# A perceiver layer on one core: another order for the first loads, the first layer norm and queries, and the combining of the weights

## The chip, the core and the metric

The kernel runs on one core of a Trainium2 chip. TensorE (PE) does the matmuls, VectorE (DVE), ScalarE (ACT) and GpSimd (POOL) the elementwise work, and SyncE (SP) issues nearly all loads. Each engine takes its instructions in the order in which the program lists them, and waits at an instruction until the semaphores that it names have been raised. The metric is the device time of one execution in microseconds (us). Before the change it is 3820.44 us (median of three runs, 3818.95 to 3823.2).

## What is computed

Sixteen sequences of 128 rows with 512 channels pass through cross attention over a context of 2048 rows each, a state space block with an MLP, and a small gated feed-forward. The change touches the first of the three:

```python
x = x + _L0_xattn_ref(_layernorm(x, axis=-1), ctx_1024, ...)
...
q = queries @ wq.T + bq
k = context @ wk.T + bk
v = context @ wv.T + bv
...
attn = jnp.einsum('bhnd,bhsd->bhns', q, k) * scale
attn = jax.nn.softmax(attn, axis=-1)
out = jnp.einsum('bhns,bhsd->bhnd', attn, v)
...
return out @ wo.T + bo
```

All values are float32.

## The kernel before, in words

**Blocks and units.** The context of each sequence is cut into four blocks of 512 rows. A block `g` yields keys (`kts`) and values (`vts`), and four units `u`, one for each group of four heads, work on it: scores (L299), maxima (L307), exponentials (L317), transposes (L330), weighted values (L343). The main loop runs over the units, and what belongs to the next block, the state space block and the MLP is put between them by tables written out by hand.

**Products.** Keys and values of a block are 512x512x512 products, made by a scheme with seven half-size products in place of eight. Weights and context are held as quarters of 2x256 columns. Four differences of context quarters, `t1` to `t4`, are formed on GpSimd (`ctx_sums`, L229), and four combinations of weight quarters, `s1` to `s4`, on VectorE (`weight_sums`, L213 to L216), the latter once for keys (`ks`) and once for values (`vs`). `product` (L237) makes one of the seven as eight passes of TensorE. They come in two phases, each in two steps: `x_products` and `y_products`. Phase 0 has products 1 and 2 in the first step, which take loaded quarters alone (`a11` with `c00`, `a12` with `c10`), and product 6 in the second; phase 1 has 7 and 5, then 3 and 4. Between them ScalarE copies a result out of PSUM (`hold`), and VectorE adds it to another (`k_sum` L257, `v_sum` L267).

**The beginning.** For block 0 there is no loop to hide in: loads, sums and products are listed one after another behind the tables (from L1128 on). SyncE's queue holds x of sequence 0 (L174), then keys' four weight quarters (L203), four context quarters (L154), values' four weight quarters, the four rows of the output projection `wo` (L169), the four columns of the query weights `wq` (L167), and the context of block 1. `wo` and `wq` share a ring of six buffers, so the last two of `wq` wait until TensorE has read two of `wo`. GpSimd issues ten small loads at the same time. All SyncE transfers of this stage are 256 KB.

The first loads are followed by the two phases of products for keys and values, with values in banks 0 and 1 of PSUM and keys in `pa` and `pc`. Then a projection of values' bias by `wo` (L464, called with `bvx`) goes to bank 2, and VectorE adds it to `bo` (L1154). Then come layer norm of sequence 0 (`moments_of`, `root_of`, `normal`: L66 to L91, L83 and L84 on ScalarE, L373), in which GpSimd adds `bo` to x (L376), the transposes of the normed rows (L385) with their copy to `xnT` (L387), and the queries (L395) with their copies to `qT` (L404). The first scores need `qT` and `kts`.

Of the kernel before, what the change touches and what calls it, by code (L numbers as in the profile page):

```python
# [10 lines left out]
ALU = mybir.AluOpType  # L11
# [23 lines left out]
def perceiver_layer(ctx: ExitStack, tc: tile.TileContext, a: dict, out: bass.AP):  # L35
    nc = tc.nc
# [72 lines left out]
    with ExitStack() as es:  # L109
# [15 lines left out]
        banks = [psum.tile([P, 512], FP, tag=f"s{j}", name=f"bank{j}") for j in range(4)]  # L125
        avp = psum.tile([P, 4, P], FP, tag="av", name="avp")
        hst = psum.tile([P, NH // 2, GT], FP, tag="h0", name="hst")
        pa = psum.tile([P, 2, 256], FP, tag="pa", name="pa")
        pc = psum.tile([P, 2, 256], FP, tag="pc", name="pc")
# [4 lines left out]
        bo = row_in(acon, "bo")  # L134
# [3 lines left out]
        ctx_t, kts, vts, qts, prs, pts, avs, stats, xts = ({} for _ in range(9))  # L138
# [5 lines left out]
        def halves(ps):  # L144
            return ps.rearrange("p (k q) -> p k q", q=256)

        def load_ctx(g, names=("c00", "c10", "c11", "c01")):

            for n in names:
                j, c = int(n[1]), int(n[2])  # L150
                t = pool.tile(
                    [P, 2, 256], FP, tag=n, name=f"{n}_{g}", bufs=1 if n == "c01" else 2
                )
                nc.sync.dma_start(  # L154
                    t,
                    a["ctxT"][g // SB, g % SB][
                        :, 2 * j : 2 * j + 2, c * 256 : (c + 1) * 256
                    ],
                )
                ctx_t[g, j, c] = t  # L160

        def load_w(i, b):

            for c in range(KC):
                t = ssm.tile([P, KC, P], FP, tag="ws", name=f"wqo{i}_{b}_{c}", bufs=WS)
                if i == 0:
                    nc.sync.dma_start(t, a["wqkvo"][i][:, :, c * P : (c + 1) * P])  # L167
                else:
                    nc.sync.dma_start(t.rearrange("p a b -> p (a b)"), a["wqkvo"][i][:, c, :])  # L169
                wts_in[i, b, c] = t  # L170

        def load_x(b):
            t = keep.tile([P, D], FP, tag="x", name=f"x{b}", bufs=4)
            nc.sync.dma_start(t, a["x"][b])  # L174
            xts[b] = t
# [20 lines left out]
            7: ("s3", "t3"),  # L196
        }

        def load_factors(of, i):

            for o, j, name in ((0, 0, "a11"), (0, 1, "a12"), (1, 1, "a22"), (1, 0, "s3")):
                t = pool.tile([P, 2, 256], FP, tag=of + name, name=of + name, bufs=1)
                nc.sync.dma_start(  # L203
                    t, a["wqkvo"][i][:, 2 * j : 2 * j + 2, o * 256 : (o + 1) * 256]
                )
                wfac[of, name] = t

        def weight_sums(of):
            a11, a12, a22, s3 = (wfac[of, n] for n in ("a11", "a12", "a22", "s3"))
            for n in ("s1", "s2", "s4"):  # L210
                wfac[of, n] = pool.tile([P, 2, 256], FP, tag=of + n, name=of + n, bufs=1)
            s1, s2, s4 = (wfac[of, n] for n in ("s1", "s2", "s4"))
            nc.vector.tensor_tensor(s1, s3, a22, ALU.add)  # L213
            nc.vector.tensor_tensor(s2, s1, a11, ALU.subtract)
            nc.vector.tensor_tensor(s3, a11, s3, ALU.subtract)
            nc.vector.tensor_tensor(s4, a12, s2, ALU.subtract)  # L216

        def ctx_sums(g, names):
            b11, b12, b21, b22 = (ctx_t[g, j, c] for j in range(2) for c in range(2))
            for n in names:  # L220
                t = pool.tile([P, 2, 256], FP, tag=n, name=f"{n}_{g}", bufs=1)
                cfac[g, n] = t
                x, y = {
                    "t1": lambda: (b12, b11),
                    "t2": lambda: (b22, cfac[g, "t1"]),
                    "t3": lambda: (b22, b12),
                    "t4": lambda: (b21, cfac[g, "t2"]),
                }[n]()
                nc.gpsimd.tensor_tensor(t, x, y, ALU.subtract)  # L229
# [41 lines left out]
        def x_products(of, g, ph, pa, pc):  # L271
            for i, ps in (((1, pa), (2, pc)), ((7, pa), (5, pc)))[ph]:
                product(of, g, i, ps)

        def hold(key, g, pa, tag):
            t = pool.tile([P, 2, 256], FP, tag=tag, name=f"{tag}{key}{g}", bufs=1)
            nc.scalar.copy(t, pa)
            held[key] = t

        def x_sums(of, g, ph, pa, pc):  # L280
            sums[of](g, ph, ph, pc, held[of])

        def y_products(of, g, ph, pa, pc):
            for i, ps in (((6, pa),), ((3, pc), (4, pa)))[ph]:
                product(of, g, i, ps)

        def y_sums(of, g, ph, pa, pc, tag="u2"):
            if ph == 0:
                hold(of + "u2", g, pa, tag)
            else:  # L290
                sums[of](g, 0, 1, pc, held[of + "u2"])
                sums[of](g, 1, 0, None, pa)
# [68 lines left out]
        def moments_of(b):  # L361
            moments(keep, mv[:, b, :], xts[b])
            xts[b, "r"] = root_first(keep, mv[:, b, 1:2], 1e-5)

        def root_of(b):
            root_second(*xts[b, "r"])

        def normal(b):

            x = xts[b]  # L370
            root_third(rstd[:, b : b + 1], *xts.pop((b, "r")))
            xn = keep.tile([P, D], FP, tag="aT", name="xn", bufs=1)
            nc.vector.tensor_scalar(  # L373
                xn, x, mv[:, b, 0:1], rstd[:, b : b + 1], ALU.subtract, ALU.mult
            )
            nc.gpsimd.tensor_tensor(x, x, bo, ALU.add)  # L376
            xts[b, "n"] = xn
            nm = [keep.tile([P, SB, 4], FP, tag=f"nm{j}", name=f"nm{b}_{j}") for j in range(4)]
            sm = keep.tile([P, SB, H], FP, tag="sm", name=f"sm{b}")
            stats[b] = nm, sm  # L380

        def turned(b, ps):
            xn = xts.pop((b, "n"))
            for kc in range(KC):
                nc.tensor.transpose(heads(ps)[:, kc, :], xn[:, kc * P : (kc + 1) * P], ident)  # L385
            xnT = keep.tile([P, KC, P], FP, tag="fx", name="xnT")
            nc.vector.tensor_copy(xnT, heads(ps))  # L387
            xts[b, "t"] = xnT

        def queries(b, ps):  # L390
            xnT = xts.pop((b, "t"))
            for oc in range(KC):
                wq = wts_in.pop((0, b, oc))
                for kc in range(KC):
                    nc.tensor.matmul(  # L395
                        heads(ps)[:, oc, :],
                        wq[:, kc, :],
                        xnT[:, kc, :],
                        start=(kc == 0),
                        stop=(kc == KC - 1),  # L400
                    )
            qT = pool.tile([P, KC, P], FP, tag="qT", name=f"qT{b}")
            for oc in range(KC):
                nc.scalar.activation(  # L404
                    qT[:, oc, :],
                    heads(ps)[:, oc, :],
                    AF.Identity,
                    bias=bq[:, oc : oc + 1],
                    scale=scale,
                )  # L410
            qts[b] = qT
# [714 lines left out]
            put(late, NU - 1, lambda ps, b=b: turned_in(xrs[b], b, "mT", ps))  # L1126


        load_x(0)
        load_factors("k", 1)  # L1130
        load_ctx(0)
        load_factors("v", 2)
        load_w(3, -1)
        nc.scalar.preload_act_table_set("natural_log_exp_and_others")
        nc.scalar.activation(aneg, aneg, AF.Exp)
        nc.vector.tensor_scalar_mul(aneg, aneg, -1.0)

        bvx = keep.tile([P, KC, P], FP, tag="fx", name="bvx")
        nc.vector.tensor_copy(bvx, bv.unsqueeze(2).to_broadcast([P, KC, P]))
        ctx_sums(0, ("t1", "t2", "t3", "t4"))  # L1140
        weight_sums("k")
        weight_sums("v")
        ways = (("k", pa, pc, "u2"), ("v", halves(banks[0]), halves(banks[1]), "u2v"))
        for ph in range(2):
            for of, sa, sc, tag in ways:
                x_products(of, 0, ph, sa, sc)
                hold(of, 0, sa, "u1")
                x_sums(of, 0, ph, sa, sc)
            for of, sa, sc, tag in ways:
                y_products(of, 0, ph, sa, sc)  # L1150
                y_sums(of, 0, ph, sa, sc, tag)
        ps = banks[2]
        out_proj(bvx, -1, ps)
        nc.vector.tensor_tensor(bo, bo, ps, ALU.add)  # L1154
        load_w(0, 0)
        load_ctx(1)
        moments_of(0)
        root_of(0)
        normal(0)
        turned(0, banks[3])  # L1160
        queries(0, banks[2])
        anew(hst)

        last = 32 * NG + LAG + 32 + 4
# [164 lines left out]
```

## Time and profile before

| | |
|---|---|
| median of three runs | 3820.44 us |
| the profiled execution's own time | 3821.1 us |
| its span | 3819.3 us |
| mean granted TensorE clock | 0.993 |
| TensorE busy from 0 to 57.60 us, before the first scores | 39.10 us |
| VectorE, ScalarE, GpSimd busy in that stretch | 18.50, 7.25, 18.84 us |
| mean rate of loads in that stretch | 142 GB/s |

The span is the time on the device from the first to the last instruction that the profiler recorded; the execution's own time holds what lies around it as well. In the timeline a row names the start in us, the length in us, the engine, the line, the operation and the tiles (written, then read), and in brackets how long the engine had been idle and what ended that. Rows of one group are merged ("x8" are eight passes), and matmuls are pipelined, so neighbouring rows overlap. A row of a window of time gives, in this order, its length, the busy time (with the number of instructions) of PE, PE's weight loads, DVE, ACT and POOL, then the granted TensorE clock, the share of DMA engines that were busy, and GB/s.

### The profile page before, as it was taken

To read this page: it belongs to the slowest core of one execution; us is meant where nothing else is said; L and a number is where in the kernel's file an instruction comes from. 1 tells how busy PE (TensorE), PEld (TensorE's weight loads), DVE (VectorE), ACT (ScalarE), POOL (GpSimd) and SP (SyncE) were. 2 spreads that over 40 slices of the span, in tenths; PEclk is the share of its full clock that TensorE was granted. 3 is DMA by queue.
4 is the path that set the end of the run, shared out by engine and by line. 5 is a ranking of instruction groups with operands and counts; after the bars stand their busy time and mean duration, and the time that the engine had idled before them with its cause. 6 is when DMAs were issued, how large, how long until landed. Compare 5 with 4: busy or idle time off the path is not lost.

```text
span 3819.3 us, 70341 instructions
## 1 busy us (share of the span) xinstructions
PE 3747.7 (98%) x26120; PEld 2856.3 (75%) x26120; DVE 2711.8 (71%) x4852; ACT 2445.3 (64%) x5847; POOL 2104.1 (55%) x1968
## 2 busy tenths in 40 slices
PE   7999999999999999999999999999999989999999
PEld 6878787778777877788778877787878766656555
DVE  3444444887878787878788778877887777677843
ACT  3555556777767776777677767776777665545421
POOL 1111113676657666765666666666675667567730
PEclk9999999999999999999999999999999999999999
DMA  3111122444353435343534453445444447577752
GB/s 92 39 38 42 45 75 65 145 141 155 121 172 133 158 119 182 130 155 115 188 125 147 129 191 123 145 131 179 135 157 131 158 169 272 193 263 257 264 191 72
DMA packets 341223, 548.40 MB, mean 144 GB/s; under 512 B 24432, under 2 KB 225408, under 8 KB 340624
## 3 DMA queue, kind: packets, MB, share of 16 engines
q1 hardware_dynamic: 340464, 543.28, 42.9%
q8 instruction: 206, 3.38, 0.3%
q14 instruction: 137, 1.12, 0.1%
q0 software_dynamic: 416, 0.63, 0.1%
HBM read 527.29 MB, written 16.52 MB: 142 GB/s over the span
## 4 chain that ended last, share of the span: by engine, by line
PE 84%; DVE 9%; ACT 3%; issue 2%; DMA 1%; POOL 1%; SPq 0%; DVEq 0%; ACTq 0%; POOLq 0%
PE pa L237 21%; PE pc L237 15%; PE bank L330 10%; PE bank L299 7%; PE avp L343 6%; PE bank L518 5%; PE bank L865 3%; PE bank L699 3%; DVE hst L670 2%; PE bank L834 2%; PE bank L960 2%; DVE nm L307 2%; PE bank L395 2%; DVE w L673 2%; PE bank L464 1%
## 5 line engine op out<-in xcount | busy, mean ns | idle before, releaser
L307 DVE TENSOR_REDUCE nm<-bank 128x1 f32<-128x512 f32 x1024 | 634.6, 681 | 251.1 <-PE bank L299 250.2
L686 POOL TENSOR_TENSOR ysum<-ysum,w 128x512 f32<-128x512 f32 x384 | 500.5, 1303 | 483.4 <-DVE hst L649 303.0
L317 ACT ACTIVATE pr<-bank,nm 128x512 f32<-128x512 f32 x1024 | 689.7, 687 | 94.6 <-DVE nm L307 89.1
L635 POOL TENSOR_TENSOR w<-dx,bc 128x512 f32<-128x512 f32 x512 | 649.7, 1290 | 3.8
L335 ACT COPY pT<-bank 128x512 f32<-128x512 f32 x816 | 437.8, 585 | 222.3 <-PE bank L330 218.1
L670 DVE TENSOR_TENSOR_SCAN hst<-hst,w 128x512 f32<-128x512 f32 x456 | 556.9, 1221 | 12.3 <-ACT hst L656 8.5
L330 PE MATMUL bank<-ident,pr 128*128 128x128 f32 x4096 | 525.8, 275 | 16.4 <-ACT pr L317 14.5
L656 ACT ACTIVATE hst<-dt,alog 128x254 f32<-128x254 f32 x912 | 436.5, 479 | 147.3 <-DVE hst L649 128.7
L330 PEld LDWEIGHTS bank<-ident,pr 128*128 128x128 f32 x4096 | 472.7, 142 | 74.7 <-ACT pr L317 22.3
L343 PEld LDWEIGHTS avp<-pT,v 128*32 128x32 f32 x8192 | 208.0, 109 | 193.7 <-issue 193.7
L673 DVE TENSOR_TENSOR w<-hst,bc 128x512 f32<-128x512 f32 x456 | 315.1, 691 | 23.7 <-DMA bc<-bcd 8.3
L299 PE MATMUL bank<-kt,qT 32*128 32x512 f32 x2048 | 297.2, 640 | 6.1 <-DVE avs L458 5.6
L229 POOL TENSOR_TENSOR t<-c,c 128x512 f32<-128x512 f32 x128 | 164.4, 1284 | 251.6 <-PE pc L237 244.4
L343 PE MATMUL avp<-pT,v 128*32 128x128 f32 x8192 | 276.7, 276 | 0.0
L237 PE MATMUL pa<-t,ks 128*128 128x256 f32 x1024 | 248.7, 386 | 0.0
L237 PE MATMUL pa<-vs,t 128*128 128x256 f32 x1008 | 244.7, 386 | 0.0
L518 PE MATMUL bank<-zT,win 128*128 128x256 f32 x968 | 222.0, 383 | 4.6 <-ACT hs L848 4.6
L237 PEld LDWEIGHTS pa<-vs,t 128*128 128x128 f32 x1008 | 185.4, 190 | 34.7 <-issue 10.1
L317 ACT ACTIVATION_READ_ACCUMULATOR pr<-bank,nm 128x1 f32 x1024 | 209.5, 205 | 0.0
L237 PEld LDWEIGHTS pa<-t,ks 128*128 128x128 f32 x1024 | 184.7, 190 | 32.6 <-issue 10.5
L333 DVE COPY pT<-bank 128x512 f32<-128x512 f32 x208 | 143.8, 691 | 89.3 <-PE bank L330 87.8
L518 PEld LDWEIGHTS bank<-zT,win 128*128 128x128 f32 x968 | 181.5, 192 | 28.7 <-ACT hs L848 5.0
(301 smaller groups left out, 6849.8 us busy)
## 6 DMA issues: line engine op xcount, KB each, us to landing
bc<-bcd SPq DMA_DIRECT2D x512, 512.0 KB, 4.3
c<-in_ctxT_dram SPq DMA_DIRECT2D x256, 256.0 KB, 4.2
wf<-in_w_dram SPq DMA_DIRECT2D x128, 512.0 KB, 7.1
wqo<-in_wqkvo_dram SPq DMA_DIRECT2D x128, 256.0 KB, 4.8
win<-in_win_dram SPq DMA_DIRECT2D x128, 256.0 KB, 4.5
wout<-in_wout_dram SPq DMA_DIRECT2D x128, 256.0 KB, 4.0
x<-in_x_dram SPq DMA_DIRECT2D x16, 256.0 KB, 3.7
x1d<-x SPq DMA_DIRECT2D x16, 256.0 KB, 2.2
```

The lines of the kernel that those rows point to most:

```text
L237: nc.tensor.matmul(ps[:, r, :], l[:, kc, r * P : (r + 1) * P], m[:, kc, :], start=(i in (1, 2, 5) and r == 0 and kc == 0), stop=(r == 1 an ...
L299: nc.tensor.matmul(banks[j], qts[b][rows, hg, :], kts[u // 4, hg][rows, :], start=True, stop=True)
L307: nc.vector.tensor_reduce(stats[b][0][j][:, sb, hg : hg + 1], banks[j], AX.X, ALU.max, negate=True)
L317: nc.scalar.activation(pr[:, j, :], banks[j], AF.Exp, bias=nm[j][:, sb, hg : hg + 1], accum_out=sm[:, sb, h : h + 1],)
L330: nc.tensor.transpose(ps[:, j, :], prs[u][:, j, i * P : (i + 1) * P], ident)
L335: nc.scalar.copy(pT, ps)
L343: nc.tensor.matmul(avp[j * HD : (j + 1) * HD, hg, :], vts[u // 4, hg // 2, i // 2][:, i % 2, hg % 2 * P + j * HD : hg % 2 * P + (j + 1) * HD],
L518: nc.tensor.matmul(ps, w[:, kc, :], zTs[g][:, kc, :], start=(kc == 0), stop=(kc == KC - 1))
L635: nc.gpsimd.tensor_tensor(w, dx.unsqueeze(1).to_broadcast([P, NH // 2, GT]), bcs[g * 32 + r, 0][:, i * NH // 2 : (i + 1) * NH // 2, :], AL ...
L656: nc.scalar.activation(bt(h[:, k, :])[:, :, 1:], bt(dt)[:, :, 1:], AF.Exp, scale=aneg[:, ec, n : n + 1],)
L670: nc.vector.tensor_tensor_scan(flat, flat, w.rearrange("p n t -> p (n t)"), 0.0, ALU.mult, ALU.add)
L686: nc.gpsimd.tensor_tensor(s, s, w, ALU.add)
```

## The change

The beginning for block 0 is listed in another order; no instruction is added or taken away.

- SyncE's queue: keys' `a11`, context `c00`, keys' `a12`, context `c10`, x, values' `a11` and `a12`, context `c11` and `c01`, keys' `s3` and `a22`, values' `s3` and `a22`, the four of `wq`, then the four of `wo`. `load_factors` takes the names of the quarters to load. Now the last two of `wo` wait for buffers of `wq`.
- Layer norm of sequence 0 stands behind the first step of keys' products, ahead of their sums.
- The first step of values' products stands ahead of the context differences and of all weight combinations. Keys' weights are combined first, then come values' first sums, and then values' weights are combined.
- Transposes and queries stand behind values' weights, ahead of the second step of phase 0. In VectorE's order the copy to `xnT` follows values' combinations; in TensorE's order the queries follow the transposes and precede product 6.
- The exponential of `alog`, its sign and `bvx` follow the queries.
- The load of `wo` follows the second step of phase 0. The projection of values' bias stays behind phase 1.
- For sequence 0 GpSimd's addition of `bo` to x leaves `normal` and follows VectorE's sum for `bo`.

From the first scores on, each engine has the same instructions in the same order as before.

```diff
-        def load_factors(of, i):
-
-            for o, j, name in ((0, 0, "a11"), (0, 1, "a12"), (1, 1, "a22"), (1, 0, "s3")):
+        QUARTERS = {"a11": (0, 0), "a12": (0, 1), "s3": (1, 0), "a22": (1, 1)}
+
+        def load_factors(of, i, names):
+
+            for name in names:
+                o, j = QUARTERS[name]
...
-            nc.gpsimd.tensor_tensor(x, x, bo, ALU.add)
+            if b:
+                nc.gpsimd.tensor_tensor(x, x, bo, ALU.add)
...
+        ways = (("k", pa, pc, "u2"), ("v", halves(banks[0]), halves(banks[1]), "u2v"))
+
+        def first_products(of, ph):
+            x_products(of, 0, ph, *dict((w[0], w[1:3]) for w in ways)[of])
+
+        def first_sums(of, ph):
+            sa, sc = dict((w[0], w[1:3]) for w in ways)[of]
+            hold(of, 0, sa, "u1")
+            x_sums(of, 0, ph, sa, sc)
+
+        load_factors("k", 1, ("a11",))
+        load_ctx(0, ("c00",))
+        load_factors("k", 1, ("a12",))
+        load_ctx(0, ("c10",))
         load_x(0)
-        load_factors("k", 1)
-        load_ctx(0)
-        load_factors("v", 2)
-        load_w(3, -1)
+        load_factors("v", 2, ("a11", "a12"))
+        load_ctx(0, ("c11", "c01"))
+        load_factors("k", 1, ("s3", "a22"))
+        load_factors("v", 2, ("s3", "a22"))
+        load_w(0, 0)
         nc.scalar.preload_act_table_set("natural_log_exp_and_others")
+        first_products("k", 0)
+        moments_of(0)
+        root_of(0)
+        normal(0)
+        first_sums("k", 0)
+        first_products("v", 0)
+        ctx_sums(0, ("t1", "t2", "t3", "t4"))
+        weight_sums("k")
+        first_sums("v", 0)
+        weight_sums("v")
+        turned(0, banks[3])
+        queries(0, banks[2])
         nc.scalar.activation(aneg, aneg, AF.Exp)
         nc.vector.tensor_scalar_mul(aneg, aneg, -1.0)
+        for of, sa, sc, tag in ways:
+            y_products(of, 0, 0, sa, sc)
+            y_sums(of, 0, 0, sa, sc, tag)
+        load_w(3, -1)
 
         bvx = keep.tile([P, KC, P], FP, tag="fx", name="bvx")
         nc.vector.tensor_copy(bvx, bv.unsqueeze(2).to_broadcast([P, KC, P]))
-        ctx_sums(0, ("t1", "t2", "t3", "t4"))
-        weight_sums("k")
-        weight_sums("v")
-        ways = (("k", pa, pc, "u2"), ("v", halves(banks[0]), halves(banks[1]), "u2v"))
-        for ph in range(2):
-            for of, sa, sc, tag in ways:
-                x_products(of, 0, ph, sa, sc)
-                hold(of, 0, sa, "u1")
-                x_sums(of, 0, ph, sa, sc)
-            for of, sa, sc, tag in ways:
-                y_products(of, 0, ph, sa, sc)
-                y_sums(of, 0, ph, sa, sc, tag)
+        for of, sa, sc, tag in ways:
+            first_products(of, 1)
+            first_sums(of, 1)
+        for of, sa, sc, tag in ways:
+            y_products(of, 0, 1, sa, sc)
+            y_sums(of, 0, 1, sa, sc, tag)
         ps = banks[2]
         out_proj(bvx, -1, ps)
         nc.vector.tensor_tensor(bo, bo, ps, ALU.add)
-        load_w(0, 0)
+        nc.gpsimd.tensor_tensor(xts[0], xts[0], bo, ALU.add)
         load_ctx(1)
-        moments_of(0)
-        root_of(0)
-        normal(0)
-        turned(0, banks[3])
-        queries(0, banks[2])
         anew(hst)
```

## The prediction, made before the changed kernel was run

> **What bounds the kernel now.** I read the page first. TensorE is busy nearly throughout and carries the chain that ended last:
>
> ```profile
> span 3819.3 us, 70341 instructions
> ...
> PE 3747.7 (98%) x26120; PEld 2856.3 (75%) x26120; DVE 2711.8 (71%) x4852; ACT 2445.3 (64%) x5847; POOL 2104.1 (55%) x1968
> ...
> PE 84%; DVE 9%; ACT 3%; issue 2%; DMA 1%; POOL 1%; SPq 0%; DVEq 0%; ACTq 0%; POOLq 0%
> ```
>
> The idle 71.6 us of TensorE (3819.3 - 3747.7) are what an edit of the order can win. The table of windows puts 18.5 us of them into the first 57.6 us (39.10 busy), where this change lies. From the first scores (L299, at 57.60) on, every engine runs the same instructions in the same order in both kernels; what the change moves ahead of them therefore shifts the whole rest. So the sum is one number: when do the first scores start? The timeline of the beginning, with start, length and what ended the idle time:
>
> ```profile
> 10.22 3.75 PE L237 MATMUL pa<-c,ka 128*128 128x256 f32 x8 [10.22 <-DMA c<-in_ctxT_dram]
> ...
> 13.89 1.78 DVE L213 TENSOR_TENSOR ks<-ks,ka 128x512 f32<-128x512 f32 x1
> ...
> 16.76 1.72 POOL L229 TENSOR_TENSOR t<-c,c 128x512 f32<-128x512 f32 x1
> ...
> 20.62 0.68 DVE L213 TENSOR_TENSOR vs<-vs,va 128x512 f32<-128x512 f32 x1
> ...
> 24.77 3.62 PE L237 MATMUL bank<-vs,t 128*128 128x256 f32 x8 [3.45 <-ACT u1v L277]
> ...
> 28.18 1.99 PE L237 MATMUL pa<-t,ks 128*128 128x256 f32 x8
> ...
> 45.73 0.69 DVE L1154 TENSOR_TENSOR bo<-bo,bank 128x512 f32<-128x512 f32 x1 [4.47 <-PE bank L464]
> ...
> 49.28 1.12 PE L385 MATMUL bank<-ident,xn 128*128 128x128 f32 x4 [3.59 <-DVE xn L373]
> ...
> 51.18 5.97 PE L395 MATMUL bank<-xnT,wqo 128*128 128x128 f32 x32 [0.78 <-DVE xnT L387]
> ...
> 57.60 1.90 PE L299 MATMUL bank<-kt,qT 32*128 32x512 f32 x8 [0.46 <-ACT qT L404]
> ```
>
> Three holes are to be seen: 10.2 us until the first context quarter lands; 3.45 us before the second group on vs (values' weights, still being combined on VectorE until 23.2); and 45.71 to 57.60, a bare chain of layer norm, transposes, queries and their copy, 11.9 us in which no product of keys or values runs.
>
> **Loads.** The issue view gives a landing for each SyncE transfer of 256 KB; by place in SyncE's queue they land at 3.4, 5.1, 7.3, 8.0, 8.7, 10.1, 12.6, 13.2, 13.7, 14.5, 15.3, 16.1, 16.8 us (places 1 to 13), then 17.5, 18.1, 18.9, 19.5 (14 to 17). The change keeps size, number and semaphore waits of the places and changes who sits in them; POOL's ten small loads beside them stay. So I give each place its old time. New first product: places 1 and 2, 5.1 (was place 6, 10.1). Second: place 4, 8.0. Values: places 6 and 7, 10.1 and 12.6. x: place 5, 8.7. ka22 and ks: 10 and 11, 15.3 (were 4 and 5, 8.7). vs and va22: 16.8. Query weights: 17.5 to 19.5.
>
> Here a rule and a row differ. The Trainium skill, DMA: Bandwidth & Descriptors, Specifications, gives about 358 GB/s of HBM to one core. By it, from the first landing at 3.4, ten more transfers and POOL's two of 256 KB take 3.15 MB / 358 = 8.8 us: place 11 at 12.2 (an estimate from that page). The rows say 15.3: in this trace 208 GB/s flow from 1.5 to 6 us, and only from 7.5 on 300 to 380. I take the rows; the rule becomes rival B.
>
> **TensorE up to the queries.** First product 5.15 to 8.6 (8 passes at the cold 0.43), the second to 10.8 or 12.0, values to about 14.3 (va12 lands 12.6, one group is 1.73), transposes of xn to about 15. VectorE has xn by then: x 8.7, BN_STATS 0.69 and the seven short steps, in all 2.9 us in the old chain (46.34 to 49.22), so 11.6. That is 5 us ahead of the old pace, and it is not kept: next in TensorE's order come the queries, which need xnT.
>
> **VectorE decides.** In its new order the copy xnT stands behind the first key sums (to about 12.5 or 13.5), four additions for keys' weights, v_00, four for values' weights.
> - Keys' additions wait for 15.3. POOL forms the four context differences from 13.75 (place 9). Where both ran side by side before, pairs took 1.67 us (VectorE ended 15.67, 17.35, 19.02, 20.69), not 0.65 as the vs additions at 20.6 to 23.2, with POOL done. Carried over: POOL's first is alone, to 15.0; its second ends 16.4, and VectorE's additions at 16.9, 18.6, 20.3, the fourth alone at 20.9.
> - v_00 0.69: 21.6. Four vs additions, 2.62: 24.25. xnT 0.69: **24.95**.
>
> So TensorE idles from 15 to 25.0.
>
> **The queries.** Warm, 32 passes take 3.57 (at 183.36 in the chain of waits). In the old beginning they took 5.97, for the granted clock was half. Clock by the windows of 1 us (the column before the last two is granted clock):
>
> ```profile
> 24.00:25.00 1.00, 0.23 (x1) 0.24 (x2) 0.27 (x2) 0.87 (x2) 0.00 (x0) 0.98 0.00 0
> 25.00:26.00 1.00, 1.00 (x3) 0.79 (x3) 0.44 (x1) 0.20 (x1) 0.00 (x0) 0.50 0.00 0
> ...
> 28.00:29.00 1.00, 1.00 (x5) 0.83 (x5) 0.00 (x0) 0.57 (x1) 0.00 (x0) 0.81 0.00 0
> ...
> 55.00:56.00 1.00, 1.00 (x8) 1.00 (x8) 0.00 (x0) 0.00 (x0) 1.00 (x2) 0.66 0.00 0
> ```
>
> After 3.45 us of idling the clock was halved for 3.4 us, after the chain at 46 to 51 for 6.8 us (48.9 to 55.7). This speaks against the change: the Trainium skill, TensorE: Matmul & The Clock Gate, What's actually happening, says that the clock halves after an idle window of about 3.4 us, recovers after a busy one, and that the windows run free of the kernel. The new gap of 10 us holds a whole window wherever these fall, so the queries start cold for certain, for 3.4 to 6.8 us. Half of the cold time is lost: by the rule 3.57 + 1.7 to 3.4 = 5.3 to 7.0; by the row 5.97. I take **6.0**. (Two old cold spells, 1.7 and 2.3 us lost, become one.)
>
> **After the queries** nothing is left to wait for: 10 groups of products and the bias projection. Before, the eight groups from 28.39 and the projection ran without a gap to 45.71 (17.32 us, so 1.73 a group and 3.45); all copies and sums between them keep the cover they had, mostly the other kind's group. 10 x 1.73 + 3.45 = 20.75. ACT's alog, moved behind the copies of qT, and VectorE's two small steps behind it wait until about 32.8, while the next key sums come at about 38: free. The last two bias quarters (wo) now wait on SyncE for the first query weights' release (about 26), and the next block's four context quarters behind them: needed at 48 and later, landing in 3 to 6 us: free. The scores need banks 0 and 1 (released as before) and bank 2, from which VectorE takes bo, 0.69 after the projection, while the first two scores run: free to 0.3. POOL's addition of bo to x moves behind it; the next context differences queue behind that and end about 7 us after the scores begin, needed at 73.3 - 57.6 = 15.7: free. ACT's square root (two steps of 0.2) precedes its u1k copy, which waits to 10.3; covered, as VectorE is behind xn until 11.6 anyway.
>
> **Sum.** 24.95 + 0.05 + 6.0 + 20.75 + 0.05 = 51.8 for the first scores, against 57.6: **5.8 us** less. The profiled execution took 3821.1 (span 3819.3 and 1.8 outside), hence **3815.3**. The median of the runs shown, 3820.44, is 0.7 below that execution; against it the gain is 5.1. Bounds: queries 5.3 to 7.0; VectorE 1 us either way; and the first scores' own cold spell (0.54 of the clock at 62.5 to 66.2, 1.7 us lost), which may be absent. That is 3813 to 3817.5.
>
> **Rivals.**
> - A, as above, 0.77.
> - B, the loads follow the rule: place 9 at 10.7, 11 at 12.2. POOL is two operations further when VectorE begins; xnT at 21.75; gain 9.0, **3812.1**. For it: 350 GB/s later in the same stage. Against: the slow start does not depend on who is loaded. 0.15.
> - C, the additions for values' weights take 1.7 as those for keys did, since loads or products, not POOL, slowed them: xnT at 29.1, gain 1.6, **3819.5**. Against: the loads end near 20 us before and after. 0.05.
> - D, slower: the clock does not come back. If after the longer gap it stays at half through all products, queries take 7.1 and the rest 41.5: scores at 73.6, **3837**. Place: L395 and L237 after the gap. With c us cold the scores start at 49.4 + c/2; from c = 16.4 the change loses. For: each restart was cold. Against: the longest cold spell seen is 6.8 us. 0.03.
>
> **Numbers.** A measurement of this kernel can tell about 0.2% from no change, 7.6 us: under 3812.8 counts as faster, over 3828.1 as slower. B is under the bound two times in three (0.10), A's lower tail 0.06: faster 0.16; slower D, 0.03; the rest 0.81. A's own range is 3813 to 3817.5; to hold eight in ten it goes on to B and part of C: 3811.5 to 3818.5.
>
> **What would show it.** First product near 5.2; ks additions from about 15.3 at 1.7 us each; xnT ending near 25 with TensorE idle for some 10 us before it; L395's 32 passes at 5.3 to 7 us and a clock of 0.50; no hole from there to the scores at 51 to 53. Wrong would make it: ks and ka22 landing well off 15.3, TensorE waiting between product groups, or the loop after the scores not keeping its pace.

## The result, and the profile after

| | before | changed |
|---|---|---|
| median of 22 runs each | 3821.66 us (3817.43 to 3823.67) | 3814.82 us (3812.92 to 3816.19) |
| ratio to before, 95% interval | | 0.9982 (0.9976 to 0.9989) |
| the profiled execution, its span | 3821.1, 3819.3 us | 3814.88, 3813.1 us |
| start of the first scores | 57.60 us | 50.63 us |
| span after that start | 3761.7 us | 3762.5 us |
| mean granted TensorE clock | 0.993 | 0.993 |

The changed kernel is 6.8 us faster by the medians. That is 0.18%, inside the 0.2% that the prediction counted as no change, though the interval leaves out 1. The forecast was 3815.3. The timeline of the beginning of the changed kernel, with columns as before:

```profile
4.77 3.75 PE L240 MATMUL pa<-c,ka 128*128 128x256 f32 x8 [4.77 <-DMA c<-in_ctxT_dram]
...
13.57 0.60 PE L389 MATMUL bank<-ident,xn 128*128 128x128 f32 x4
...
14.29 1.63 DVE L216 TENSOR_TENSOR ks<-ks,ka 128x512 f32<-128x512 f32 x1 [3.04 <-DMA ka<-in_wqkvo_dram]
...
15.34 1.71 POOL L232 TENSOR_TENSOR t<-c,c 128x512 f32<-128x512 f32 x1
...
20.39 0.68 DVE L216 TENSOR_TENSOR vs<-vs,va 128x512 f32<-128x512 f32 x1
...
22.91 0.69 DVE L391 COPY xnT<-bank 128x512 f32<-128x512 f32 x1
...
23.65 6.35 PE L399 MATMUL bank<-xnT,wqo 128*128 128x128 f32 x32 [9.48 <-DVE xnT L391]
29.84 1.89 PE L240 MATMUL pa<-t,ks 128*128 128x256 f32 x8
...
50.63 1.98 PE L302 MATMUL bank<-kt,qT 32*128 32x512 f32 x8
```

Of TensorE's three holes the first has shrunk to 4.77 us, and in place of the other two there is one of 9.48 us ahead of the queries. Its row names VectorE's copy `xnT` as what ended it. From the queries to the scores no row of products has a bracket: there TensorE never waits. The table of windows shows what the hole costs beside its own length:

```profile
14.20:18.50 4.30, 0.00 (x0) 0.00 (x0) 4.17 (x3) 0.00 (x0) 4.30 (x3) 1.00 1.20 304
18.50:23.60 5.10, 0.00 (x0) 0.00 (x0) 5.06 (x8) 0.00 (x0) 0.21 (x1) 0.52 0.27 92
23.60:28.50 4.90, 4.85 (x22) 4.85 (x23) 0.00 (x0) 0.00 (x0) 0.00 (x0) 0.50 0.19 56
28.50:30.00 1.50, 1.50 (x12) 1.50 (x12) 0.00 (x0) 0.00 (x0) 0.00 (x0) 0.85 0.72 173
```

While TensorE has nothing, VectorE is busy throughout: 3 operations in 4.17 us beside GpSimd, then the rest of the third and seven more in 5.06 us once GpSimd is done. The clock column falls to half in the second window and stays there for the first 5.3 us of the queries: the 4.9 us of the third window, and, since the last one averages 0.85, some 0.4 us of that (0.15 x 1.5 / 0.5). Half of it, about 2.6 us, is lost. On the page each engine has as many instructions as before:

```profile
span 3813.1 us, 70343 instructions
...
PE 3745.4 (98%) x26120; PEld 2854.8 (75%) x26120; DVE 2711.9 (71%) x4852; ACT 2449.0 (64%) x5847; POOL 2105.6 (55%) x1968
...
PE 85%; DVE 9%; ACT 3%; issue 2%; DMA 1%; POOL 0%; DVEq 0%; SPq 0%; ACTq 0%
```

TensorE is idle for 67.7 us (3813.1 - 3745.4) against 71.6.

Of the 6.97 us won up to the first scores, 0.8 are missing at the end of this one execution. Nothing in the traces ties them to the change. TensorE's matmuls from the scores on are the same in both kernels (elsewhere a few small operations slip from ahead of the scores to behind their start: two of VectorE, the sum for `bo` and a memset, and five of GpSimd, `bo` added to x and the next block's differences). Set side by side, matmul by matmul, the two traces keep within 0.22 us of each other from 15 to 3040 us behind the first scores; the 0.8 us arise after that, where all half-clock spells behind the scores but the first lie.

Other executions differ there too. Over all twelve traces on record the span after the scores lies between 3759.6 and 3764.4 us. By and large it is longer where the granted clock stood at half for longer (3759.6 us with 27.4 us in `diff_on_vector`, 3760.5 with 34.1 in `warm_gap2`, 3762.5 with 39.7 in the changed kernel, 3764.4 with 44.4 in `copy_early`), but not always: `order_only` has 3759.6 with 37.5, and before has more of it than the changed kernel, 43.1, and a shorter span, 3761.7. What makes the rest of the difference is open. So below the start of the scores, which one trace gives to a tenth, is set beside the medians, which average over this.

### The profile page after: what moved, and what is told of

Same layout as the page of the kernel before. It is cut to its first block, busy times and chain, and to the rows that moved or that the text cites. A ratio compares the mean times of both kernels' runs of the same rounds, so it can differ in the third digit from the quotient of the medians.

```text
span 3813.1 us, 70343 instructions
## 1 busy us (share of the span) xinstructions
PE 3745.4 (98%) x26120; PEld 2854.8 (75%) x26120; DVE 2711.9 (71%) x4852; ACT 2449.0 (64%) x5847; POOL 2105.6 (55%) x1968
## 4 chain that ended last, share of the span: by engine, by line
PE 85%; DVE 9%; ACT 3%; issue 2%; DMA 1%; POOL 0%; DVEq 0%; SPq 0%; ACTq 0%
PE pa L240 21%; PE pc L240 16%; PE bank L333 10%; PE bank L302 7%; PE avp L346 6%; PE bank L522 5%; PE bank L869 4%; PE bank L703 3%; DVE hst L674 2%; PE bank L838 2%; DVE nm L310 2%; PE bank L964 2%; PE bank L399 2%; DVE w L677 2%; PE bank L468 1%
```

## The experiments

The theory: the order of work alone makes the gain, and VectorE's list decides when the queries can start, since `xnT` stands behind eight additions. The rivals: the new loads make the gain; what slows VectorE is the loads and products beside it (rival C); the halved clock, not the wait, is what the hole costs. "Before" beside each median is before's own median, measured along with it on the same chip.

### Loads alone, order alone

`loads_only` has before's order of work with the changed kernel's list of loads; `order_only` is the reverse.

```diff
 # loads_only, on before
-        load_x(0)
-        load_factors("k", 1)
-        load_ctx(0)
-        load_factors("v", 2)
+        load_factors("k", 1, ("a11",)); load_ctx(0, ("c00",))
+        load_factors("k", 1, ("a12",)); load_ctx(0, ("c10",))
+        load_x(0)
+        load_factors("v", 2, ("a11", "a12")); load_ctx(0, ("c11", "c01"))
+        load_factors("k", 1, ("s3", "a22")); load_factors("v", 2, ("s3", "a22"))
         load_w(3, -1)
 # order_only, on the changed kernel: the loads again in the old order
+        load_x(0)
+        load_factors("k", 1, ("a11", "a12", "a22", "s3")); load_ctx(0)
+        load_factors("v", 2, ("a11", "a12", "a22", "s3"))
         load_w(0, 0)
```

> The new order of the loads alone (the first query weights stay behind the bias projection, as before); work in the old order. Theory (VectorE's chain decides, the loads bring little by themselves): the first product starts near 5, values' first products end near 13.5, but VectorE still forms both sets of weights before any sum, the keys' from 14.3 and the values' to about 22.5, and the second group on vs starts near 24 instead of 24.8; the bare chain of norm and queries stays. First scores at 56 to 57.5, time 0 to 1.5 us under the kernel before. Rival (the gain is the earlier first product): 4 to 5 us under the kernel before.

> The new order of the work alone; the loads stand in the old order, except that the query weights precede the output projection's, which the new order needs. Theory: first product near 10.2, key sums to about 17, key weights' additions from there, mostly beside POOL's last two or three differences, xnT near 25, scores near 52: 1 to 2 us slower than the changed kernel, about 5 us under the kernel before. Rival (the gain is the earlier first product): no more than 1 or 2 us under the kernel before. The landing times of this run and of loads_only also tell whether the earlier landings (14.2 for the eleventh transfer against 15.3) go with the order of the loads or with the run.

`loads_only`: 3821.64 us (before 3821.69), ratio 1.0001 (0.9993 to 1.0009). `order_only`: 3815.26, ratio 0.998 (0.9972 to 0.9989). The timeline of `loads_only`:

```profile
4.77 3.47 PE L240 MATMUL pa<-c,ka 128*128 128x256 f32 x8 [4.77 <-DMA c<-in_ctxT_dram]
...
18.10 3.63 PE L240 MATMUL pa<-t,ks 128*128 128x256 f32 x8 [4.67 <-DVE ks L217]
...
24.29 3.23 PE L240 MATMUL bank<-vs,t 128*128 128x256 f32 x8 [2.56 <-ACT u1v L280]
...
57.33 1.90 PE L302 MATMUL bank<-kt,qT 32*128 32x512 f32 x8 [0.46 <-ACT qT L407]
```

and that of `order_only`:

```profile
10.31 3.75 PE L240 MATMUL pa<-c,ka 128*128 128x256 f32 x8 [10.31 <-DMA c<-in_ctxT_dram]
...
24.18 0.68 DVE L391 COPY xnT<-bank 128x512 f32<-128x512 f32 x1
24.91 5.46 PE L399 MATMUL bank<-xnT,wqo 128*128 128x128 f32 x32 [4.71 <-DVE xnT L391]
...
51.01 1.98 PE L302 MATMUL bank<-kt,qT 32*128 32x512 f32 x8
```

In the first, TensorE starts 5.5 us earlier and the scores start 0.3 us earlier: the head start is waited away, 4.67 us of it ahead of product 6 of keys on `ks`, the rest ahead of product 6 of values, which starts at 24.29 where it was 24.77. In the second, TensorE starts as late as before, and the scores start at 51.01, 0.38 us from the changed kernel (1 to 2 us were expected). The order of work makes nearly the whole gain. The loads are worth nothing that the times can tell, with either order of work. The traces show a little more: with the old loads `xnT` is there at 24.86, with the new ones at 23.60. But the hole ahead of the queries is shorter with the old loads, and the queries behind it took 5.46 us in place of 6.35, so most of these 1.3 us did not reach the scores. How much of that is chance in the clock, these runs do not tell.

### Why the transfers came sooner than forecast

In the changed kernel `ks` and `ka22` had landed at 14.2 us where 15.3 was forecast. One thing that places alone do not keep is which tile goes first. In `x_first` x takes the head of the queue again:

```diff
+        load_x(0)
         load_factors("k", 1, ("a11",))
         load_ctx(0, ("c00",))
         load_factors("k", 1, ("a12",))
         load_ctx(0, ("c10",))
-        load_x(0)
```

> The changed kernel with x as the first transfer; the other loads keep their order behind it. It tells why the places land about 1 us earlier with the new loads. If x at the head makes the slow start, the third transfer lands near 7.3 and the eleventh near 15.3 as before the change; if four quarters of one weight in a row make it, they land near 6.2 and 14.2 as after it. The time is not expected to move by more than 1 us.

One execution took 3813.77 us, with the scores at 50.99. From the DMA view of the first 60 us (slices of 1.5 us, GB/s of all loads together), `x_first` and then the changed kernel:

```profile
GB/s 0 216 214 213 255 256 380 321 344 350 322 292 305 251 20 0 0 0 25 184 197 324 311 330 38 0 0 0 0 0 0 153 22 0 0 0 0 0 63 112
```

```profile
GB/s 0 186 261 316 257 320 369 331 351 342 298 291 344 74 0 0 0 34 149 173 285 344 349 75 0 0 0 0 0 0 0 175 0 0 0 0 0 0 134 41
```

The third and fourth slice (3 to 6 us) carry 214 and 213 with x at the head, 261 and 316 without. The third transfer of the queue landed at 7.0 us here, 7.3 before and in `order_only`, and 5.8 to 6.2 in three without x at the head. The first key addition began at 15.80 where it was 14.29. So x at the head costs the queue some 0.8 to 1.5 us, which is the size of the 1.1 us that the forecast lacked. `x_first` is a single execution, but the traces of before and of `order_only`, with x at the head too, agree with it. The scores moved by 0.36 us only, as the queries took 5.21 us. Why x is slower is open: x is 128 rows of 2 KB, the other tiles are two pieces of 1 KB per partition, and no run changed that alone.

### What slows the additions

In `diff_on_vector` the first block's context differences run on VectorE instead of GpSimd, amid the same loads:

```diff
-                nc.gpsimd.tensor_tensor(t, x, y, ALU.subtract)
+                eng = nc.gpsimd if g else nc.vector
+                eng.tensor_tensor(t, x, y, ALU.subtract)
```

> The changed kernel with the first block's four context differences on VectorE instead of POOL. Theory (keys' additions take 1.67 because POOL works beside them): all eight take 0.6 to 0.7, from about 12.8; keys' weights done near 18.3, xnT near 22, queries 1.5 us earlier, time about 1.5 us under the changed kernel. Rival (the loads that still land slow VectorE's additions): each takes 1.6 until about 19.7, xnT near 26, time 2 us over the changed kernel.

It took 3811.2 us (before 3821.69), ratio 0.9972 (0.996 to 0.9983). The timeline:

```profile
13.69 0.69 DVE L233 TENSOR_TENSOR t<-c,t 128x512 f32<-128x512 f32 x1
...
15.50 0.68 DVE L216 TENSOR_TENSOR ks<-ks,ka 128x512 f32<-128x512 f32 x1
...
18.63 0.68 DVE L216 TENSOR_TENSOR vs<-vs,va 128x512 f32<-128x512 f32 x1
...
21.90 5.62 PE L400 MATMUL bank<-xnT,wqo 128*128 128x128 f32 x32 [7.66 <-DVE xnT L392]
...
48.16 1.98 PE L303 MATMUL bank<-kt,qT 32*128 32x512 f32 x8
```

A key addition takes 0.68 us at 15.50, with the loads still running, against 1.63 in the changed kernel; TensorE idles beside it in both. GpSimd beside VectorE makes the difference; loads and products do not, and rival C falls. It is cheaper to give VectorE the four differences too (four of 0.6) than to let three of its additions run a microsecond longer each: `xnT` ends 1.76 us earlier (21.84 against 23.60), and the scores start 2.5 us earlier. In the medians it cannot be told from the changed kernel (the intervals overlap).

### The price of the clock

`warm_gap` fills the hole with 70 transposes of the identity matrix into the queries' bank, `warm_gap2` with 84; their results are not used.

```diff
         turned(0, banks[3])
+        for _ in range(70):
+            nc.tensor.transpose(heads(banks[2])[:, 0, :], ident, ident)
         queries(0, banks[2])
```

> The changed kernel with 70 more passes of TensorE, identity by identity into the bank of the queries, which overwrite them, in the gap before the queries; nothing waits for them. Theory (the queries are slow because the gap of 9.5 us halves the clock): they end before xnT is there, the clock stays at 1.0, the queries take 3.6 to 3.9 instead of 6.35, and the time falls by about 2.7 us under the changed kernel, to about 3812. Rival (they are slow for their weight loads): no change, within 0.5 us.

> As warm_gap with 84 passes instead of 70, so that the gap before the queries, still 2.2 us there, is under 1 us. Theory (the halved clock makes the queries slow, and in warm_gap the rest of the gap still halved it, 1.5 us into the queries): queries at 3.6 to 3.9, time 2.3 to 2.8 us under the changed kernel. Rival: queries at 5.3 or more as in warm_gap.

`warm_gap` took 3813.41 us (before 3821.69), ratio 0.9977 (0.9968 to 0.9986). Its timeline and its windows:

```profile
14.09 7.80 PE L1166 MATMUL bank<-ident 128*128 128x128 f32 x70
...
24.09 5.47 PE L399 MATMUL bank<-xnT,wqo 128*128 128x128 f32 x32 [2.20 <-DVE xnT L391]
```

```profile
21.80:24.10 2.30, 0.10 (x2) 0.01 (x1) 2.23 (x4) 0.00 (x0) 0.00 (x0) 1.00 0.00 0
24.10:25.50 1.40, 1.40 (x12) 1.40 (x13) 0.00 (x0) 0.00 (x0) 0.00 (x0) 0.95 0.00 0
25.50:28.60 3.10, 3.10 (x16) 3.10 (x16) 0.00 (x0) 0.00 (x0) 0.00 (x0) 0.50 0.41 121
28.60:30.00 1.40, 1.40 (x11) 1.35 (x10) 0.00 (x0) 0.41 (x2) 0.00 (x0) 0.94 0.74 198
```

The expectation of 3.6 to 3.9 us for the queries was missed, by the filler's length: a hole of 2.20 us was left, and the clock halved not in it but 1.3 us into the queries, at 25.35, for 3.4 us (3.1 in the third window, 0.14 and 0.17 in its neighbours by their means of 0.95 and 0.94). `warm_gap2` leaves no hole. It took 3811.15 us (before 3820.5), ratio 0.9976 (0.9967 to 0.9986):

```profile
15.14 9.33 PE L1166 MATMUL bank<-ident 128*128 128x128 f32 x84
...
24.32 3.74 PE L399 MATMUL bank<-xnT,wqo 128*128 128x128 f32 x32
```

At full clock the queries take 3.74 us, so of the changed kernel's 6.35 us 2.6 are the cold clock. The scores start at 48.69, 1.9 us ahead of the changed kernel's (behind the fillers the queries start 0.4 us after `xnT`). So the cold clock is a part of what the hole costs; its own 9.48 us are the larger one. In the medians the fillers cannot be told from the changed kernel (the intervals overlap).

### Another place for the queries, and for the copy

Two ways lead past the hole. In `queries_late` the queries go behind the second phase of products, where `xnT` is long there:

```diff
         turned(0, banks[3])
-        queries(0, banks[2])
...
+        queries(0, banks[3])
         ps = banks[2]
         out_proj(bvx, -1, ps)
```

In `copy_early` they stay, and the transposes with VectorE's copy `xnT` go ahead of the weight combinations:

```diff
         first_products("v", 0)
+        turned(0, banks[3])
         ctx_sums(0, ("t1", "t2", "t3", "t4"))
         weight_sums("k")
         first_sums("v", 0)
         weight_sums("v")
-        turned(0, banks[3])
         queries(0, banks[2])
```

`copy_early_v` has the copy early, behind the context differences, which are on VectorE as in `diff_on_vector`; `copy_early_wq` is `copy_early` with the loads of the query weights ahead of the last two of values' (`load_w(0, 0)` ahead of `load_factors("v", 2, ("s3", "a22"))`).

> The changed kernel with the queries (not the transposes and the copy xnT) moved behind the second phase of products, ahead of the bias projection, in bank 3. Theory (what is lost is the gap before the queries, not the queries' own work): TensorE goes on with product 6 of keys at about 17.6 and that of values near 22.5, all else follows without a gap, queries warm in 3.6; first scores near 45 and a time about 5.5 us under the changed kernel. Rival (layer norm off the end of the beginning is all that counts, the queries' place does not): within 1 us of the changed kernel.

> The changed kernel with the transposes of the normed rows and their copy to xnT listed right behind values' first products, so that on VectorE the copy stands ahead of both sets of weights. Theory (the gap before the queries is the copy's place behind the weights on VectorE): xnT near 15, the queries then wait for their weights only (landing 16.7 to 19.5) and end near 20.5, product 6 of keys follows at once, that of values near 22 to 23; first scores at 41 to 43 instead of 50.6 and a time 8 to 9.5 us under the changed kernel. Rival (the additions for values' weights hold TensorE anyway, or the gap only moves): less than 3 us.

> The context differences of the first block on VectorE and the copy to xnT right behind them, ahead of both sets of weights. Theory: xnT near 16.3, queries bound by their weights' landing as in copy_early and ended near 20.5, values' weights ready near 21.5 and thus no wait for them; first scores near 41, time 0 to 1 us under copy_early. Rival (VectorE still binds): 1.5 us or more under copy_early.

> As copy_early, with the four loads of query weights ahead of the last two quarters of values' weights. Theory (in copy_early the queries start when their weights land, at 17.0, while xnT is there at 16.1): start at 16.1 to 16.3, values' weights still in time, time 0.5 to 0.9 us under copy_early, hardly to be told from it. Rival (values' weights become late): 1 us or more over copy_early.

| | median, us | before, us | ratio to before | first scores, us |
|---|---|---|---|---|
| changed | 3814.82 | 3821.66 | 0.9982 (0.9976 to 0.9989) | 50.63 |
| queries_late | 3811.35 | 3821.66 | 0.9973 (0.9963 to 0.9983) | 46.28 |
| copy_early | 3804.69 | 3820.5 | 0.9958 (0.9946 to 0.9971) | 41.50 |
| copy_early_v | 3805.19 | 3820.5 | 0.996 (0.9946 to 0.9973) | 41.27 |
| copy_early_wq | 3805.87 | 3821.66 | 0.9959 (0.9945 to 0.9972) | 41.58 |

The timeline of `queries_late`:

```profile
18.58 3.75 PE L240 MATMUL pa<-t,ks 128*128 128x256 f32 x8 [3.28 <-DVE ks L217]
...
22.78 2.75 PE L240 MATMUL bank<-vs,t 128*128 128x256 f32 x8 [0.45 <-DVE vs L217]
...
39.18 3.73 PE L399 MATMUL bank<-xnT,wqo 128*128 128x128 f32 x32
...
46.28 1.98 PE L302 MATMUL bank<-kt,qT 32*128 32x512 f32 x8
```

The queries run at full clock, and product 6 starts 11 us earlier than in the changed kernel. But the hole has not gone. What is left of it, 3.28 us, has moved ahead of product 6, and the products behind it are cold in place of the queries (3.75 and 2.75 us for a group that takes 1.89 at 29.84 in the changed kernel). The scores start at 46.28 where about 45 was expected, and in the medians it cannot be told from the changed kernel (5.5 us less were expected). The timeline of `copy_early`:

```profile
15.37 0.69 DVE L391 COPY xnT<-bank 128x512 f32<-128x512 f32 x1 [2.96 <-PE bank L389]
...
17.04 3.81 PE L399 MATMUL bank<-xnT,wqo 128*128 128x128 f32 x32 [1.71 <-DMA wqo<-in_wqkvo_dram]
...
22.42 1.91 PE L240 MATMUL bank<-vs,t 128*128 128x256 f32 x8
...
41.50 1.98 PE L302 MATMUL bank<-kt,qT 32*128 32x512 f32 x8
```

The copy costs VectorE the same 0.69 us. It is not quite free there: the keys' quarter `a22` has landed near 14.5, and the key additions start behind the copy, at 15.98; but the queries on TensorE now run beside them. The queries wait for their own weights, 1.71 us, not for VectorE; they run at full clock, and cover the weight combinations. The scores start 9.1 us earlier than in the changed kernel, 6.6 because the queries start earlier and 2.5 because they are warm, and the intervals of the two ratios lie apart. `copy_early` beats both kernels, by 0.4% and about 0.25% of the time.

What binds next was tried from two sides. In `copy_early_v` the queries still wait for their weights and start 0.2 us earlier:

```profile
16.83 3.81 PE L400 MATMUL bank<-xnT,wqo 128*128 128x128 f32 x32 [2.14 <-DMA wqo<-in_wqkvo_dram]
...
41.27 1.98 PE L303 MATMUL bank<-kt,qT 32*128 32x512 f32 x8
```

and `copy_early_wq` starts them at 16.07, only to wait later:

```profile
16.07 3.84 PE L399 MATMUL bank<-xnT,wqo 128*128 128x128 f32 x32 [0.78 <-DVE xnT L391]
...
22.44 1.97 PE L240 MATMUL bank<-vs,t 128*128 128x256 f32 x8 [0.80 <-DVE vs L217]
```

Product 6 of values starts at 22.42 in `copy_early` and 22.44 here: the microsecond won ahead of the queries is waited away on `vs`. The three can't be told apart. Both edits together were not tried.

## Why the prediction was right

It held in its mechanism and in its sum, the latter with two terms off in opposite directions.

- **The three holes of before**: one reading was off, without touching the sum. The 3.45 us ahead of product 6 of values (the first group on `vs`, not the second) were not ended by values' weights, done at 23.22, but by ScalarE's copy `u1v`, done at 24.71, and that waited for VectorE's key sums, which are listed behind values' weights:

```profile
24.13 0.58 ACT L277 COPY u1v<-bank 128x512 f32<-128x512 f32 x1 [9.53 <-DVE kt L257]
```

- **"When do the first scores start?"** The reduction of the change to this one number held: 6.97 us won there, 6.2 in the execution and 6.8 by the medians.
- **"I give each place its old time"** was 1.1 us too late. Place 3 landed at 6.15 (7.3 forecast), 9 near 12.7 (13.7), 11 at 14.2 (15.3). The step took the slow start for a property of the queue; `x_first` shows that about that much of it came with x at its head, which the change moves. Rival B's rule would have had place 11 at 12.2, further off than the rows: B falls, with the true value about a third of the way to it. (B's remark that GpSimd is two operations further does not follow from its landings, which are 1.5 us apart as the rows' are 1.6; its `xnT` at 21.75 comes from the earlier landing alone.)
- **"That is 5 us ahead of the old pace, and it is not kept"**: shown by `loads_only`, with a first product at 4.77 and a ratio of 1.0001.
- **"VectorE decides"**: from the loads to `xnT` 9.65 us were forecast (15.3 to 24.95) and 9.4 taken (14.2 to 23.60). Additions beside GpSimd took 1.63 to 1.74 us (1.67 forecast), alone 0.68. That GpSimd is the cause, which the forecast carried over from one overlap, is shown by `diff_on_vector`; rival C falls.
- **The queries** took 6.35 us where 6.0 was chosen between 5.3 and 7.0. The cold spell came, as argued. Its share of the queries, 5.3 us here, differs from run to run and not with the length of the hole alone: in `order_only`, with a hole of 4.71 us, they took 5.46, in `diff_on_vector`, with 7.66, 5.62, in `x_first`, with 8.55, 5.21. So that 6.0 came so near is in part luck.
- **"After the queries nothing is left to wait for"**: 20.75 us forecast, 20.79 measured (29.84 to 50.63). Rival D falls, as the clock was back at 28.95 us.
- **The sum**: the scores at 51.8 forecast and 50.63 measured. VectorE 1.35 us earlier, queries 0.35 later, and the small joints the rest. The late part of the loop, where executions differ, then took back 0.8 us in this one. That is luck: it put the total (3814.88 in the profiled execution, 3815.3 forecast) nearer to the forecast than its parts were.

What the forecast saw and did not follow up is that the hole of 10 us came from one line: the copy `xnT` listed behind eight additions that it doesn't need. `copy_early` shows that this place alone (with that of the transposes ahead of it) held back 9 us, more than the change itself won.

## What to carry to other kernels

When a step is moved forward, look up where its operand is produced in the other engine's order: it comes no earlier than everything listed ahead of it there. Loads that arrive sooner win nothing while a later step on the same engine waits for something else. That a row names a transfer as what ended a wait is not enough: before's first product did (10.22 us), and `loads_only` removed 5.5 us of that wait and won nothing. A hole ahead of matmuls costs its length and a spell of halved clock behind it, and moving work out of it may only hand both to the next group.

## What the runs showed of the hardware

- A hole of 2.20 us, followed by 1.3 us of matmuls, was enough to halve the clock for 3.4 us (`warm_gap`). The Trainium skill, TensorE: Matmul & The Clock Gate, What's actually happening, speaks of an idle window of about 3.4 us; here none was whole. TensorE need not even have idled for half of such a stretch: in the changed kernel it was busy for 1.88 of the 3.41 us ahead of the spell that begins at 56.25, amid the first maxima and exponentials. Which share of busy time decides is open.

```profile
52.84:56.25 3.41, 1.88 (x11) 1.31 (x12) 1.43 (x3) 2.99 (x10) 3.33 (x3) 1.00 0.00 0
56.25:59.66 3.41, 3.41 (x15) 1.94 (x13) 0.05 (x1) 1.68 (x4) 1.54 (x2) 0.50 0.24 77
```

- VectorE's additions of two 128x512 float32 tiles took 0.68 us alone and 1.63 to 1.74 us beside GpSimd's in the changed kernel, which themselves went from 1.26 to 1.71 us. The Trainium skill, GPSIMD Engine Reference, Specifications, names this contention for VectorE instructions with two inputs in SBUF, without a size.
- From 3 to 6 us all loads together ran at 213 to 214 GB/s with x at the head of SyncE's queue and at 261 to 316 without (`x_first` and the changed kernel).
- The same matmuls from the first scores on took 3759.6 to 3764.4 us in twelve executions, by and large longer where the records show more time at half clock.
